# A gated cross-attention block with a mixture of experts: the first batch brought alone to its scores, the rest of its block behind it

## The chip, the cores and the metric

The kernel runs on one core of a Trainium2 chip. The core has five engines that work side by side and wait for each other through semaphores: TensorE (PE, matrix products, with PEld for its weight loads), VectorE (DVE), ScalarE (ACT), GpSimd (POOL) and SyncE (SP, which here only issues transfers). The metric is the device time of one execution in microseconds (us); a comparison takes the median of several runs. One execution is also recorded by the hardware profiler, and all rows quoted here are from such a record.

## The reference

Inputs are `x` of 16 batches x 128 rows x 128 features, a context of 16 x 77 x 96, and the weights, all in 32-bit floats. Cut to what matters:

```python
# 1. gated cross-attention, 16 heads of 8 features
h  = layernorm(x)
q  = h @ Wq.T + bq                       # [16, 128, 16 heads, 8]
kv = ctx_768 @ Wkv.T + bkv               # per head 8 key and 8 value features
k, v = kv[..., :8], kv[..., 8:]
att = softmax(q k^T / sqrt(8), over the 77 context rows)
x  = x + tanh(g_xattn) * ((att @ v) @ Wo.T + bo)
# 2. gated mixture of experts, 4 rounds, 4 experts, the best 2 of each row
cur = layernorm(x)
for r in range(4):
    w   = softmax of the two largest of (cur @ Wg[r] + bg[r]), zero elsewhere
    cur = cur + sum_e w[e] * (gelu(cur @ W1[e] + b1[e]) @ W2[e] + b2[e])
out = x + tanh(g_ffn) * cur
```

## The kernel before, in words

The 16 batches are tiles of 128 rows. They are prepared in four blocks of four (`BB = 4`, `NB = 4`): normalization, turning (transposing) `x` and the context, keys, queries and values are done for a block at a time. The order of the instructions on PE, DVE and ACT is the order of the program text (a manual schedule); POOL's is kept in program order too, by the wrapper `gp`. An engine takes its instructions strictly one after the other, so an instruction that waits holds up all behind it on that engine.

**The head, up to line 876.** Loads are issued from three queues: SP brings `x` and the context block by block, ACT the projection weights, and POOL the two bias rows of `wkT` and `wvT`. DVE clears both `vm` buffers (the values, spread out with zeros, one for even and one for odd blocks) and makes `hmask`, which picks a head's rows. `warm(n)` puts n products of a zero matrix on PE. Then, for the first block: `Wkv` and `Wq` are turned, and the first four contexts (`turn_ctx(0)`); `keys(0)` makes `kT`; `cols` is made by turning `cols_n`, the expert biases `b1` with the query bias `bq` as a last row; `stats_x` and `Norm.scale` find mean and 1/deviation for four tiles (the power -1/2 is taken on POOL); `norm_x(0)` applies them on DVE; `turn_x(0)` and `queries(0)` make `qT`. `spread_keys(b)` multiplies `kT` with `hmask` (`km`, on POOL), so that `scores(b)` can compute four heads by one product. `weights` is the softmax without its division: largest value (`mx`) and difference (`ex`) on DVE, exponential on ACT, in two halves. `values(0)` makes `vm[0]`. In the same stretch the second block's statistics and norm, its contexts and its keys are placed.

`spread_rows` (line 878) spreads small rows over all partitions: gate weights' biases, the two gates (`tg`), the attention's output bias (`bo_b`), and turns `Wo` and `Wg`. All its results lie in one PSUM bank.

**The attention loop, line 1039.** One turn for each batch b. A turn makes `km` of batch b+2, turns the weights of batch b (`turn_weights`, PE into `ps_tr`, copied by ACT to `exT`), makes the scores of b+1 between the two halves of that, starts the softmax of b+1, and multiplies the weights of b with ones and values (`attend`, `ps_av`); `over_sums` divides (`rs`, `oT`), and `put_out` of the next turn adds the result to `x`. Work of the later blocks and of the routing is hung into the turns by hand, through lists of functions at four places of a turn:

```python
    early[1] += [lambda: turn_x(1)]
    extra[2] += [lambda: queries(1)]
    extra[3] += [lambda: values(1)]
    for b in (0, 1, 2, 5, 6):
        behind[b] += [lambda: advance(constants, 1)]
```

`early` comes after the first half of the turned weights, `extra` after the second half, `amid` after `attend`, and `behind` at the end of the turn. `constants` are tables for the routing, made on POOL in five steps.

**PSUM.** The pool `p_m` (`bank`) has two banks, used in turn by nearly all products; `p_tr` (`bank_tr`) has two for `ps_tr`; `p_sc` (`banks2`) has two pairs for scores, which `warm` uses too. A bank is given to the next user when its last reader is done.

**The experts, from line 1082.** Eight phases (two halves of the rows, four rounds) go over pieces of 128 rows sorted by expert: two layers on PE (`ps_h`, `ps_y`), the gelu on ACT.

Of the kernel before, what the change touches and what calls it, by code (L numbers as in the profile page):

```python
# [31 lines left out]
P = 128  # L32
# [14 lines left out]
def gated_xattn_moe(  # L47
# [66 lines left out]
    def bank(name):  # L114
        return p_m.tile([P, 512], F32, tag="m", name=name)
# [3 lines left out]
    ctx_sb = keep.tile([M, B, C], F32, name="ctx_sb")  # L119
    wkv_n = const.tile([P, 2, C], F32, name="wkv_n")  # L120
    wq_n = const.tile([D, D], F32, name="wq_n")
    NCOL = E * NF + 1
    cols_n = const.tile([NCOL, P], F32, name="cols_n")

    wkT = const.tile([C + 1, D], F32, name="wkT")
    wvT = const.tile([C + 1, D], F32, name="wvT")

    nc.scalar.dma_start(wkv_n, Wkv.rearrange("(t p) c -> p t c", p=P))
    nc.scalar.dma_start(wq_n, Wq)
    wg_sb = const.tile([D, R, E], F32, name="wg_sb")  # L130
    nc.scalar.dma_start(wg_sb, Wg.rearrange("r d e -> d r e"))
    nc.scalar.dma_start(cols_n[E * NF : NCOL, :], bq.rearrange("(o d) -> o d", o=1))
    nc.scalar.dma_start(cols_n[0 : E * NF, :], b1.rearrange("e (c p) -> (e c) p", p=P))
    bkv_v = bkv.rearrange("(o h t d) -> o t h d", o=1, t=2, d=DH)
    ident = const.tile([P, P], F32, name="ident")
    make_identity(nc, ident)
    for t, w in ((0, wkT), (1, wvT)):
        gp.dma_start(
            w[C : C + 1, :].rearrange("o (h d) -> o h d", d=DH), bkv_v[:, t]
        )  # L140
    for i in range(NB):
        nc.sync.dma_start(
            x_sb[:, ts(i, BB), :], x[ts(i, BB)].rearrange("b l d -> l b d")
        )
        nc.sync.dma_start(
            ctx_sb[:, ts(i, BB), :], ctx_768[ts(i, BB)].rearrange("b m c -> m b c")
        )
# [51 lines left out]
    nc.vector.tensor_reduce(
        hmask,  # L200
        ident.rearrange("p (g k d) -> p k g d", k=HG, d=DH),
        AX.XY,
        ALU.add,
    )
# [475 lines left out]
    warm(9)  # L680
    ps = bank("ps_wkv")
    for t in range(2):
        tp(ps[:C, ts(t, P)], wkv_n[:, t, :], ident)
    tp(ps[:, 2 * P : 3 * P], wq_n, ident)
    for t, w in ((0, wkT), (1, wvT)):
        nc.vector.tensor_copy(
            w[0:C, :].rearrange("c (h d) -> c h d", d=DH),
            ps[:C, : 2 * D].rearrange("c (h t d) -> c t h d", t=2, d=DH)[:, t],
        )
    wqT = const.tile([D, D], F32, name="wqT")  # L690
    nc.scalar.copy(wqT, ps[:, 2 * P : 3 * P])
# [33 lines left out]

    xnTs = {}

    def turn_x(i):
        ps = bank("ps_xt")
        for j in range(BB):  # L730
            tp(ps[:, ts(j, P)], row(i * BB + j, 0, D), ident)
        xnTs[i] = awork.tile([P, TB], F32, tag="xnT", name="xnT")
        nc.scalar.copy(xnTs[i], ps)

    def queries(i):
        ps = bank("ps_q")
        mm(ps, wqT, xnTs.pop(i), start=True, stop=True)
        nc.scalar.activation(qT[i], ps, AF.Identity, bias=bqc)

    def values(i):  # L740
        ps = bank("ps_v")
# [94 lines left out]
    def put_out(b, oT, bank):  # L836
# [30 lines left out]
    warm(10)
    turn_x(0)
    warm(3)
    queries(0)  # L870
    warm(4)
    scs = scores(0, kms.pop(0))
    values(0)
    turn_ctx(1)
    ex = {0: weights(scs)}
    keys(1)

    def spread_rows():
# [7 lines left out]
        nc.scalar.activation(tg, rows_b[:, R * E : NROW], AF.Tanh)
        nc.vector.tensor_scalar(bo_b, ps[:, ts(1, D)], tg[:, 0:1], None, ALU.mult)
        nc.scalar.copy(woT, ps[:, ts(2, D)])
        wgT = const.tile([R * E, D], F32, name="wgT")
# [147 lines left out]
    extra[B - 1] += [begin]  # L1037
    o = {}
    for b in range(B):
        if b + 2 < B:  # L1040
            kms[b + 2] = spread_keys(b + 2)
        exT = awork.tile([M, NH, L], F32, tag="exT", name="exT")
        turn_weights(ex[b], exT, (0, 1))
        for f in early[b]:
            f()
        if b + 1 < B:
            scs = scores(b + 1, kms.pop(b + 1))
        turn_weights(ex.pop(b), exT, (2, 3))
# [29 lines left out]
        if b == 14:  # L1078
            load(0, stores)
# [280 lines left out]
```

## Time and profile before

| what | value |
|---|---|
| three runs | 449.91, 449.91 and 450.17 us; median 449.91 |
| the profiled execution | 448.24 us, of it 446.4 from the first to the last instruction (the span) |
| busy over the span | PE 430.0, DVE 346.5, ACT 274.8, POOL 214.4 us |
| mean granted clock of TensorE | 0.994 |
| head: up to the first turn's first `ps_tr` | 19.4 us |
| attention loop | 19.4 to about 114 us |
| experts | from about 114 us on |

In the rows below a number in front is the start in microseconds from the span's start, then the duration, the engine, the line, the instruction, what it writes and reads, and how often; in brackets the idle time before it and what ended it. A matrix product of 32-bit floats appears as two instructions (passes). PE's weight loads have rows of their own (PEld). Rows of the same group that follow each other are merged into one.

### The profile page before, as it was taken

How to read it: one execution, taken by the hardware profiler on the slowest of the kernel's cores; microseconds unless marked ns; L12 is line 12 of the kernel's file. 1: busy time of each engine (PE TensorE's matmuls, PEld its weight loads, DVE VectorE, ACT ScalarE, POOL GpSimd, SP SyncE). 2: the span in 40 equal slices, each digit the busy share in tenths (PEclk: the TensorE clock that was granted, in tenths of full speed). 3: DMA queues.
4: the chain of work that ended last, by engine and by line, in shares of the span. 5: the costliest groups of instructions: out<-in, count | busy, mean ns of one | idle time of the engine just before them, and what ended most of it. 6: DMA issues, size and time to landing. Idle time of an engine off the chain costs nothing.

```text
span 446.4 us, 12234 instructions
## 1 busy us (share of the span) xinstructions
PE 430.0 (96%) x4506; PEld 405.3 (91%) x4506; DVE 346.5 (78%) x918; ACT 274.8 (62%) x853; POOL 214.4 (48%) x249
## 2 busy tenths in 40 slices
PE   6899999998999999999999999999999999999991
PEld 6677888877899999999999999999999999999991
DVE  8489998998866996897698689858867986774561
ACT  2567766766655666566666656666665666666661
POOL 5561926157005934752592377158426814650061
PEclk9999999999999999999999999999999999999997
DMA  7520000012202301300130122014002201410000
GB/s 166 184 96 4 1 3 1 1 40 76 84 3 74 121 2 51 122 28 3 72 123 1 38 73 88 1 63 135 2 26 73 98 3 63 134 42 8 1 35 14
DMA packets 19553, 24.08 MB, mean 54 GB/s; under 512 B 3940, under 2 KB 16550, under 8 KB 19366
## 3 DMA queue, kind: packets, MB, share of 16 engines
q1 hardware_dynamic: 14868, 13.41, 9.6%
q0 software_dynamic: 3648, 9.71, 6.0%
q8 instruction: 36, 0.59, 0.5%
q10 hardware_dynamic: 978, 0.18, 0.2%
q14 instruction: 23, 0.19, 0.1%
HBM read 13.58 MB, written 9.71 MB: 52 GB/s over the span
## 4 chain that ended last, share of the span: by engine, by line
PE 71%; issue 9%; DVE 8%; POOL 6%; DMA 4%; ACT 1%; POOLq 0%; ACTq 0%; DVEq 0%
PE ps_y L262 28%; PE ps_h L262 28%; POOL out_dram L1124 4%; PE ps_av L262 4%; PE ps_tr L265 4%; DVE mx L791 2%; DMA wall<-in_L_ffn_W_dram 2%; DVE ex L795 2%; PE ps_c L265 2%; DVE rs L831 1%; PE sc L262 1%; DMA ctx_sb<-in_ctx_dram 1%; PE ps_bh L262 1%; DMA wq_n<-in_L_xattn_Wq_dram 1%; ACT exT L809 1%
## 5 line engine op out<-in xcount | busy, mean ns | idle before, releaser
L1096 ACT ACTIVATE hT<-ps_h,wb 128x128 f32<-128x128 f32 x512 | 145.9, 368 | 81.6 <-ACT hT L1096 56.7
L262 PE MATMUL ps_h<-curT,wb 128*128 128x128 f32 x1024 | 135.4, 275 | 0.7 <-ACT curT L379 0.7
L262 PE MATMUL ps_y<-wb,hT 128*128 128x128 f32 x1024 | 135.7, 276 | 0.0
L262 PEld LDWEIGHTS ps_h<-curT,wb 128*128 128x128 f32 x1024 | 124.6, 192 | 0.9 <-ACT curT L379 0.9
L262 PEld LDWEIGHTS ps_y<-wb,hT 128*128 128x128 f32 x1024 | 124.5, 192 | 0.0
L522 POOL DMA_INDIRECT sorted<-rows,pos_i x64 | 69.9, 1092 | 112.2 <-DVE start L515 49.3
L1015 DVE COPY wb<-wall 128x1028 f32 x128 | 105.4, 826 | 12.7 <-issue 6.5
L93 POOL TENSOR_TENSOR lp<-rows,wg_rows 128x512 f32<-128x512 f32 x48 | 75.3, 1593 | 29.7 <-DVE rows L1110 27.5
L1110 DVE SCALAR_TENSOR_TENSOR rows<-ps_y,pws,rows 128x128 f32<-128x128 f32 x126 | 43.6, 346 | 33.9 <-PE ps_y L262 33.9
L1096 ACT ACTIVATE hT<-ps_h,wall 128x128 f32<-128x128 f32 x160 | 45.7, 368 | 32.6 <-PE ps_h L262 32.6
L262 PE MATMUL ps_y<-wall,hT 128*128 128x128 f32 x320 | 43.1, 278 | 0.0
L262 PE MATMUL ps_h<-cx,wall 128*128 128x128 f32 x320 | 42.3, 275 | 0.0
L809 ACT COPY exT<-ps_tr 77x512 f32<-77x512 f32 x64 | 34.0, 581 | 13.4 <-PE ps_tr L265 13.1
L262 PEld LDWEIGHTS ps_y<-wall,hT 128*128 128x128 f32 x320 | 38.9, 192 | 2.7 <-ACT hT L1096 2.7
L262 PEld LDWEIGHTS ps_h<-cx,wall 128*128 128x128 f32 x320 | 38.9, 192 | 0.0
L265 PEld LDWEIGHTS ps_tr<-ident,ex 128*77 128x77 f32 x256 | 27.9, 147 | 10.1 <-ACT exT L809 7.8
L265 PE MATMUL ps_tr<-ident,ex 128*77 128x128 f32 x256 | 35.1, 280 | 1.1 <-ACT exT L809 1.1
L1124 POOL DMA_INDIRECT out_dram<-res,id_i x16 | 18.5, 1158 | 35.8 <-DVE res L1115 31.8
L419 DVE TENSOR_REDUCE lg<-lp 128x4 f32<-128x512 f32 x48 | 32.3, 674 | 3.4 <-POOL lp L93 3.4
L801 ACT ACTIVATE ex<-ex 128x616 f32<-128x616 f32 x32 | 23.0, 719 | 13.7 <-DVE ex L795 13.4
L791 DVE TENSOR_REDUCE mx<-sc 128x8 f32<-128x616 f32 x32 | 25.3, 790 | 5.8 <-PE sc L262 5.7
L795 DVE TENSOR_TENSOR ex<-sc,mx 128x616 f32<-128x616 f32 x32 | 25.4, 794 | 1.5
(170 smaller groups left out, 450.9 us busy)
## 6 DMA issues: line engine op xcount, KB each, us to landing
rows<-sorted SPq DMA_DIRECT2D x16, 528.0 KB
x_sb<-in_x_dram SPq DMA_DIRECT2D x4, 256.0 KB
wall<-in_L_ffn_W_dram SPq DMA_DIRECT2D x1, 1024.0 KB
wall<-in_L_ffn_W_dram SPq DMA_DIRECT2D x4, 256.0 KB
wg_rows<-wg_turned SPq DMA_DIRECT2D x1, 1024.0 KB
sorted<-rows,pos_i POOLq DMA_INDIRECT x64, 2.6
ctx_sb<-in_ctx_dram SPq DMA_DIRECT2D x4, 115.5 KB
out_dram<-res,id_i POOLq DMA_INDIRECT x16, 2.3
```

The costliest lines, as they stand in the source:

```text
L93: return lambda *a, **kw: tc.keep_in_program_order(f(*a, **kw))
L262: nc.tensor.matmul(*args, **kw)
L265: nc.tensor.transpose(*args)
L419: nc.vector.tensor_reduce(lgs[h][:, t, :], prods.pop((h, t)), AX.X, ALU.add)
L522: ins = nc.gpsimd.indirect_dma_start(out=sorted_rows[h], out_offset=bass.IndirectOffsetOnAxis(ap=pos_i[:, t : t + 1], axis=0), in_=rows[h] ...
L791: beats.append(nc.vector.tensor_reduce(mx, sv, AX.X, ALU.max))
L795: nc.vector.tensor_tensor(eu.rearrange("l (g h) m -> l g h m", h=HG), sv, mx.unsqueeze(3).to_broadcast([P, 2, HG, M]), ALU.subtract,)
L809: nc.scalar.copy(exT[:, ts(g, HG), :].rearrange("m h l -> m (h l)"), ps[:M, :])
L1015: nc.vector.tensor_copy(wb, wall[:, ds(e, 1), :].rearrange("p o n -> p (o n)"))
L1096: nc.scalar.activation(hT[:, fc, :], ps[:, ts(fc, P)], AF.Gelu_apprx_tanh, bias=wb[:, W_B + fc : W_B + fc + 1],)
L1110: return nc.vector.scalar_tensor_tensor(at, y, w, at, ALU.mult, ALU.add)
L1124: ins = nc.gpsimd.indirect_dma_start(out=out_rows, out_offset=bass.IndirectOffsetOnAxis(ap=id_i[:, t : t + 1], axis=0), in_=res, in_offset ...
```

## The change: what it does

It rearranges the head and the first turns of the loop.

- Loads. SP brings `x` of batch 0 alone first, then the first block's contexts, the other three tiles of `x`, then `wg_sb` and `b1` (both from ACT's queue before), then the later blocks. ACT's queue brings `Wkv`, the two bias rows (from POOL's queue before), `Wq`, and `bq` as a column by itself.
- A copy of one element (`junk`) is put ahead of ACT's other work.
- The norm of the first block is split: tile 0, tile 1, tiles 2 and 3, each with its own scale. Tiles 0 and 1 are applied on DVE, 2 and 3 on POOL. `turn_x` and `queries` take a range of tiles: tile 0, then tile 1, and in turn 0 of the loop tiles 2 and 3.
- `km` of batch 0 is made on DVE. Keys and queries of tile 0 come before `scores(0)`; queries of tile 1 stand in front of `values(0)`, and the copies of the values behind the softmax of batch 0.
- `warm(9)`, `warm(2)`, `warm(10)`, `warm(3)`, `warm(4)` become `warm(6)` and groups of 1 to 4 zero products (`warm_tr`, in `p_tr`'s banks) between the steps: 19 in place of 28.
- Into the loop move: `turn_ctx(1)` (turn 0), `keys(1)` (turn 1), `spread_rows`, `residual(0)`, and statistics and norm of block 1 (end of turn 0), the clearing of `vm[1]`, now on POOL (end of turn 0). `turn_x(1)` goes from turn 1 to turn 2, the routing constants' first three steps go one turn later, and two statistics of block 2 from turn 0 to turn 1. `km` of batch 3 is made at the end of turn 0. `blk` is cleared on POOL later, just ahead of the expert loads.
- `b1` is turned within `spread_rows`, in its bank, and copied from there to `wall`.

```diff
-    NCOL = E * NF + 1
-    cols_n = const.tile([NCOL, P], F32, name="cols_n")
+    cols_n = const.tile([E * NF, P], F32, name="cols_n")
+    bqc = const.tile([P, 1], F32, name="bqc")
...
     nc.scalar.dma_start(wkv_n, Wkv.rearrange("(t p) c -> p t c", p=P))
+    for t, w in ((0, wkT), (1, wvT)):
+        nc.scalar.dma_start(w[C : C + 1, :].rearrange("o (h d) -> o h d", d=DH), bkv_v[:, t])
     nc.scalar.dma_start(wq_n, Wq)
-    nc.scalar.dma_start(wg_sb, Wg.rearrange("r d e -> d r e"))
-    nc.scalar.dma_start(cols_n[E * NF : NCOL, :], bq.rearrange("(o d) -> o d", o=1))
-    nc.scalar.dma_start(cols_n[0 : E * NF, :], b1.rearrange("e (c p) -> (e c) p", p=P))
+    nc.scalar.dma_start(bqc, bq.rearrange("(d o) -> d o", o=1))
-    for t, w in ((0, wkT), (1, wvT)):
-        gp.dma_start(
-            w[C : C + 1, :].rearrange("o (h d) -> o h d", d=DH), bkv_v[:, t]
-        )
-    for i in range(NB):
+    nc.sync.dma_start(x_sb[:, 0, :], x[0])
+    nc.sync.dma_start(ctx_sb[:, 0:BB, :], ctx_768[0:BB].rearrange("b m c -> m b c"))
+    nc.sync.dma_start(x_sb[:, 1:BB, :], x[1:BB].rearrange("b l d -> l b d"))
+    nc.sync.dma_start(wg_sb, Wg.rearrange("r d e -> d r e"))
+    nc.sync.dma_start(cols_n, b1.rearrange("e (c p) -> (e c) p", p=P))
+    for i in range(1, NB):
...
-    for i in range(2):
-        nc.vector.memset(vm[i], 0.0)
+    nc.vector.memset(vm[0], 0.0)
...
-    gp.memset(blk, 0.0)
...
+    junk = const.tile([1, 1], F32, name="junk")
+    nc.scalar.copy(junk, zero[0:1, 0:1])
+    def warm_tr(n):
+        ps = bank_tr("ps_warm")
+        for _ in range(n):
+            mm(ps[:, :P], zero, zero, start=True, stop=True)
...
+    def turn_wq():
+        ps = bank_tr("ps_wq")
+        tp(ps[:, :P], wq_n, ident)
+        nc.scalar.copy(wqT, ps[:, :P])
...
-    turn_ctx(0)
-    warm(2)
-    keys(0)
-    ps = bank("ps_cols")
-    tp(ps[:, :NCOL], cols_n, ident[:NCOL, :NCOL])
-    nc.scalar.copy(cols, ps[:, :NCOL])
-    nc.scalar.copy(
-        wall[:, :, W_B:WW], cols[:, 0 : E * NF].rearrange("p (e c) -> p e c", c=NF)
-    )
-    for j in range(BB):
-        stats_x(0, j)
-    norms[0].scale()
-    kms = {0: spread_keys(0), 1: spread_keys(1)}
-    stats_x(1, 0)
-    stats_x(1, 1)
-    norm_x(0, nc.vector)
-    stats_x(1, 2)
-    stats_x(1, 3)
-    norms[1].scale()
-    norm_x(1, gp)
-    load_experts()
-    warm(10)
-    turn_x(0)
-    warm(3)
-    queries(0)
-    warm(4)
-    scs = scores(0, kms.pop(0))
-    values(0)
-    turn_ctx(1)
-    ex = {0: weights(scs)}
-    keys(1)
+    norms0 = Norm(1, "b"), Norm(1, "c"), Norm(BB - 2, "d")
+    norms0[0].stats(0, x_sb[:, 0, :])
+    norms0[0].scale()
+    nc.vector.tensor_reduce(
+        hmask, ident.rearrange("p (g k d) -> p k g d", k=HG, d=DH), AX.XY, ALU.add
+    )
+    warm(6)
+    norms0[0].apply(0, row(0, 0, D), x_sb[:, 0, :], nc.vector)
+    turn_wkv()
+    turn_ctx(0)
+    warm_tr(1)
+    turn_wq()
+    turn_x(0, 0, 1)
+    warm_tr(2)
+    norms0[1].stats(0, x_sb[:, 1, :])
+    norms0[1].scale()
+    keys(0)
+    warm_tr(1)
+    queries(0, 0, 1)
+    warm_tr(3)
+    for j in range(2, BB):
+        norms0[2].stats(j - 2, x_sb[:, j, :])
+    norms0[2].scale()
+    kms = {0: spread_keys(0, nc.vector), 1: spread_keys(1)}
+    norms0[1].apply(0, row(1, 0, D), x_sb[:, 1, :], nc.vector)
+    scs = scores(0, kms.pop(0))
+    turn_x(0, 1, 2)
+    warm_tr(2)
+    queries(0, 1, 2)
+    values(0, False)
+    warm_tr(4)
+    ex = {0: weights(scs)}
+    values_done(0)
+    for j in range(2, BB):
+        norms0[2].apply(j - 2, row(j, 0, D), x_sb[:, j, :], gp)
+    gp.memset(blk, 0.0)
+    load_experts()
...
-    spread_rows()
-    residual(0)
-    early[1] += [lambda: turn_x(1)]
+    def spread_more():
+        kms[3] = spread_keys(3)
+    extra[0] += [lambda: turn_x(0, 2, BB), lambda: queries(0, 2, BB), lambda: turn_ctx(1)]
+    extra[1] += [lambda: keys(1)]
+    behind[0] += [spread_rows, spread_more, lambda: residual(0)]
+    for j in range(BB):
+        behind[0] += [lambda j=j: stats_x(1, j)]
+    behind[0] += [lambda: norms[1].scale(), lambda: norm_x(1, gp), lambda: gp.memset(vm[1], 0.0)]
+    early[2] += [lambda: turn_x(1)]
     extra[2] += [lambda: queries(1)]
     extra[3] += [lambda: values(1)]
-    for b in (0, 1, 2, 5, 6):
+    for b in (1, 2, 3, 5, 6):
         behind[b] += [lambda: advance(constants, 1)]
...
-            behind[b - 4 + j] += [lambda i=i, j=j: stats_x(i, j)]
+            behind[max(b - 4 + j, 1)] += [lambda i=i, j=j: stats_x(i, j)]
```

More of the change, by code (lines that the diff above doesn't have):

```diff
@@ L128, in gated_xattn_moe @@
     nc.scalar.dma_start(wkv_n, Wkv.rearrange("(t p) c -> p t c", p=P))
+    wg_sb = const.tile([D, R, E], F32, name="wg_sb")
+    bkv_v = bkv.rearrange("(o h t d) -> o t h d", o=1, t=2, d=DH)
+    for t, w in ((0, wkT), (1, wvT)):
+        nc.scalar.dma_start(w[C : C + 1, :].rearrange("o (h d) -> o h d", d=DH), bkv_v[:, t])
     nc.scalar.dma_start(wq_n, Wq)
-    wg_sb = const.tile([D, R, E], F32, name="wg_sb")
-    nc.scalar.dma_start(wg_sb, Wg.rearrange("r d e -> d r e"))
-    nc.scalar.dma_start(cols_n[E * NF : NCOL, :], bq.rearrange("(o d) -> o d", o=1))
-    nc.scalar.dma_start(cols_n[0 : E * NF, :], b1.rearrange("e (c p) -> (e c) p", p=P))
-    bkv_v = bkv.rearrange("(o h t d) -> o t h d", o=1, t=2, d=DH)
+    nc.scalar.dma_start(bqc, bq.rearrange("(d o) -> d o", o=1))
     ident = const.tile([P, P], F32, name="ident")
     make_identity(nc, ident)
-    for t, w in ((0, wkT), (1, wvT)):
-        gp.dma_start(
-            w[C : C + 1, :].rearrange("o (h d) -> o h d", d=DH), bkv_v[:, t]
-        )
-    for i in range(NB):
+    nc.sync.dma_start(x_sb[:, 0, :], x[0])
[4 more added lines that the diff above has]
+    for i in range(1, NB):
         nc.sync.dma_start(
@@ L195, in gated_xattn_moe @@
     vm = [akeep.tile([M, BB, HG * (D + DH)], F32, name=f"vm{i}") for i in range(2)]
-    for i in range(2):
-        nc.vector.memset(vm[i], 0.0)
[L199 to L203, printed above, removed]
-    )
+    nc.vector.memset(vm[0], 0.0)
     ctxT = akeep.tile([C + 1, B, M], F32, name="ctxT")
@@ L677, in warm, with turn_wkv @@
             mm(ps[:, 0, :P], zero, zero, start=True, stop=True)
[L680 to L689, printed above, removed]
-    wqT = const.tile([D, D], F32, name="wqT")
-    nc.scalar.copy(wqT, ps[:, 2 * P : 3 * P])
+    junk = const.tile([1, 1], F32, name="junk")
+    nc.scalar.copy(junk, zero[0:1, 0:1])
+    wqT = const.tile([D, D], F32, name="wqT")
+    def warm_tr(n):
+        ps = bank_tr("ps_warm")
+        for _ in range(n):
+            mm(ps[:, :P], zero, zero, start=True, stop=True)
+    def turn_wkv():
+        ps = bank("ps_wkv")
+        for t in range(2):
+            tp(ps[:C, ts(t, P)], wkv_n[:, t, :], ident)
+        for t, w in ((0, wkT), (1, wvT)):
+            nc.vector.tensor_copy(
+                w[0:C, :].rearrange("c (h d) -> c h d", d=DH),
+                ps[:C, : 2 * D].rearrange("c (h t d) -> c t h d", t=2, d=DH)[:, t],
+            )
[3 more added lines that the diff above has]
+        nc.scalar.copy(wqT, ps[:, :P])
     kT = akeep.tile([D, B, M], F32, name="kT")
     qT = [akeep.tile([D, TB], F32, name=f"qT{i}") for i in range(NB)]
-    cols = const.tile([P, NCOL], F32, name="cols")
-    bqc = cols[:, E * NF : NCOL]
     norms = {}
@@ L726, in gated_xattn_moe, with turn_x, queries, values @@
     xnTs = {}
-    def turn_x(i):
+    def turn_x(i, lo=0, hi=BB):
         ps = bank("ps_xt")
-        for j in range(BB):
+        for j in range(lo, hi):
             tp(ps[:, ts(j, P)], row(i * BB + j, 0, D), ident)
+        at = slice(lo * P, hi * P)
         xnTs[i] = awork.tile([P, TB], F32, tag="xnT", name="xnT")
-        nc.scalar.copy(xnTs[i], ps)
-    def queries(i):
+        nc.scalar.copy(xnTs[i][:, at], ps[:, at])
+    def queries(i, lo=0, hi=BB):
         ps = bank("ps_q")
[L737 to L741, printed above, removed]
+        at = slice(lo * P, hi * P)
+        mm(ps[:, at], wqT, xnTs.pop(i)[:, at], start=True, stop=True)
+        nc.scalar.activation(qT[i][:, at], ps[:, at], AF.Identity, bias=bqc)
+    pss_v = {}
+    def values(i, done=True):
+        ps = pss_v[i] = bank("ps_v")
         for j in range(BB):
             mm(ps[:M, ts(j, D)], ctxT[:, i * BB + j, :], wvT, start=True, stop=True)
+        if done:
+            values_done(i)
+    def values_done(i):
+        ps = pss_v.pop(i)
         for j in range(BB):
@@ L751, in values, with spread_keys @@
             )
-    def spread_keys(b):
+    def spread_keys(b, eng=gp):
         km = awork.tile([D, HG, M], F32, tag="km", name="km")
-        gp.tensor_tensor(
+        eng.tensor_tensor(
             km,
@@ L843, in put_out @@
         )
-    turn_ctx(0)
-    warm(2)
-    keys(0)
-    ps = bank("ps_cols")
-    tp(ps[:, :NCOL], cols_n, ident[:NCOL, :NCOL])
-    nc.scalar.copy(cols, ps[:, :NCOL])
-    nc.scalar.copy(
-        wall[:, :, W_B:WW], cols[:, 0 : E * NF].rearrange("p (e c) -> p e c", c=NF)
-    )
-    for j in range(BB):
-        stats_x(0, j)
-    norms[0].scale()
-    kms = {0: spread_keys(0), 1: spread_keys(1)}
-    stats_x(1, 0)
-    stats_x(1, 1)
-    norm_x(0, nc.vector)
-    stats_x(1, 2)
-    stats_x(1, 3)
-    norms[1].scale()
-    norm_x(1, gp)
-    load_experts()
-    warm(10)
-    turn_x(0)
-    warm(3)
-    queries(0)
-    warm(4)
-    scs = scores(0, kms.pop(0))
-    values(0)
-    turn_ctx(1)
-    ex = {0: weights(scs)}
-    keys(1)
+    norms0 = Norm(1, "b"), Norm(1, "c"), Norm(BB - 2, "d")
[3 more added lines that the diff above has]
+        hmask, ident.rearrange("p (g k d) -> p k g d", k=HG, d=DH), AX.XY, ALU.add
+    )
+    warm(6)
+    norms0[0].apply(0, row(0, 0, D), x_sb[:, 0, :], nc.vector)
+    turn_wkv()
+    turn_ctx(0)
+    warm_tr(1)
[4 more added lines that the diff above has]
+    norms0[1].scale()
+    keys(0)
+    warm_tr(1)
[17 more added lines that the diff above has]
+    gp.memset(blk, 0.0)
+    load_experts()
     def spread_rows():
@@ L882, in spread_rows @@
         mm(ps[:, ts(1, D)], ones, bo_row, start=True, stop=True)
+        tp(ps[:, 32 : 32 + E * NF], cols_n, ident[: E * NF, : E * NF])
         tp(ps[:, ts(2, D)], wo_n, ident)
@@ L888, in spread_rows @@
         nc.scalar.copy(woT, ps[:, ts(2, D)])
+        nc.scalar.copy(
+            wall[:, :, W_B:WW],
+            ps[:, 32 : 32 + E * NF].rearrange("p (e c) -> p e c", c=NF),
+        )
         wgT = const.tile([R * E, D], F32, name="wgT")
@@ L1039, in gated_xattn_moe @@
     for b in range(B):
-        if b + 2 < B:
+        if b + 2 < B and b + 2 not in kms:
             kms[b + 2] = spread_keys(b + 2)
@@ L1063, in gated_xattn_moe @@
         if b == B - 1:
-            junk = const.tile([1, 1], F32, name="junk")
             nc.scalar.activation(junk, zero[0:1, 0:1], AF.Gelu_apprx_tanh)
```

## The prediction

> **What bounds the kernel now.** The page first: busy time of each engine.
>
> ```profile
> PE 430.0 (96%) x4506; PEld 405.3 (91%) x4506; DVE 346.5 (78%) x918; ACT 274.8 (62%) x853; POOL 214.4 (48%) x249
> ```
>
> TensorE (PE) is the long engine, but where it idles or only multiplies zeros decides here. So next the busy time by stretch (columns: stretch, its length, then PE, PEld, DVE, ACT, POOL).
>
> ```profile
> 0.00:20.00 20.00, 15.75 (x106) 13.13 (x107) 13.05 (x35) 6.72 (x17) 10.34 (x23) 1.00 0.71 195
> 20.00:66.00 46.00, 45.42 (x754) 36.15 (x753) 40.82 (x87) 33.04 (x66) 24.38 (x79) 1.00 0.07 25
> 112.00:440.00 328.00, 324.50 (x2952) 320.23 (x2941) 249.99 (x693) 204.78 (x714) 156.68 (x121) 1.00 0.16 53
> ```
>
> From 20 us on PE is full (45.42 of 46, 324.5 of 328), so microseconds won before it shift everything behind. Between 66 and 112 the chain of waits runs through VectorE (DVE), but it starts at the row `rs` at 65.92, which waits for PE: that stretch shifts too. What counts is when the first batches get through, so the timeline of the head (start, duration, engine, line, operation):
>
> ```profile
> 6.29 1.28 ACT L691 ACT_TABLE_LOAD   x1 [6.29 <-DVE wvT L686]
> 8.10 1.04 POOL L93 TENSOR_TENSOR rstda<-rstda,half 128x4 f32<-128x4 f32 x1 [3.44 <-DVE rstda L251]
> 9.18 1.91 DVE L255 TENSOR_SCALAR rows<-x_sb,mva,rstda 128x128 f32<-128x128 f32 x4 [0.35 <-POOL rstda L93]
> 11.45 0.60 PE L265 MATMUL ps_xt<-ident,rows 128*128 128x128 f32 x4
> 12.72 1.12 PE L262 MATMUL ps_q<-xnT,wqT 128*128 128x512 f32 x2
> 14.72 0.87 PE L262 MATMUL sc<-km,qT 32*128 32x308 f32 x8
> 15.54 0.80 DVE L791 TENSOR_REDUCE mx<-sc 128x8 f32<-128x616 f32 x1 [3.44 <-PE sc L262]
> 19.40 1.04 PE L265 MATMUL ps_tr<-ident,ex 128*77 128x128 f32 x8
> 20.05 0.35 DVE L887 TENSOR_SCALAR bo_b<-ps_rows,tg 128x128 f32<-128x128 f32 x1 [0.27 <-ACT tg L886]
> 20.49 0.27 ACT L888 COPY woT<-ps_rows 128x128 f32<-128x128 f32 x1 [0.47 <-PE ps_tr L265]
> 25.11 1.10 PE L265 MATMUL ps_tr<-ident,ex 128*77 128x128 f32 x8
> 30.98 1.10 PE L265 MATMUL ps_tr<-ident,ex 128*77 128x128 f32 x8
> 36.74 1.10 PE L265 MATMUL ps_tr<-ident,ex 128*77 128x128 f32 x8
> ```
>
> The first softmax (`mx`) starts at 15.54, after four tiles were normed, turned and multiplied. Turn 0 of the attention loop begins with its first `ps_tr` at 19.40, turns 1, 2, 3 at 25.11, 30.98, 36.74. Rows L691 and L888 show a habit of this kernel: ScalarE (ACT) starts reading a PSUM bank only when DVE, ahead of it in the program, has finished with that bank. Last the waits; SyncE's tell when loads landed:
>
> ```profile
> SPq L145 <- DMA wkv_n<-in_L_xattn_Wkv_dram: 1.7, 1, 1.7
> SPq L145 <- DMA wq_n<-in_L_xattn_Wq_dram: 0.2, 1, 0.2
> ```
>
> The issues behind these waits ran at 3.85 and 4.84, so `wkv_n` (96 KB, issued 0.72) landed at 3.8 and `wq_n` (64 KB, issued 1.25) at 4.8.
>
> **The change, step by step.** I walk the new order with durations of this profile.
>
> *Norm of tile 0.* `x[0]` (64 KB, first on SP, issued near 0.73) lands between 3.0 (by the stretches of 1 us, the first 250 KB of all loads had moved by then) and 3.85, the time of the larger `wkv_n`; I take 3.4, and DVE's first `vm` fill ends at 3.4 anyway. Statistics 0.45 and scale 0.17 (rows at 6.14 and 7.84), power 1.04 on GpSimd (POOL, free by 2.9 since the two bias loads left it), one apply 0.34: 5.5. The `wkT` and `wvT` copies follow (0.46): 6.0. They hold the PSUM bank that `turn_x` needs, so PE turns x at 6.1. `turn_wq` lies ahead: `wq_n` is now ACT's fourth load, issued near 2.3 instead of 1.25; 3.6 us later is 5.9, just hidden. If it takes 1 us longer, that is 1 us lost. The table load (1.28) moves to about 3.2 on an idle ACT: hidden.
>
> *PE to the scores.* Turn 0.27, two zero products 0.50 (a product is two passes of 0.125: 20 passes in 2.50 at 9.11), keys 0.76, one more 0.25, queries of one tile 0.40 (a 128x128 product pair takes 0.38 to 0.49), three more 0.75: 9.0. Beside it `kT` is copied by 8.1 and `qT` by 8.7. The new `spread_keys(0)` on DVE costs 0.40, half of `ex` (616 elements, 0.80). Its bound is the neighbour: in the row at 9.18 two of the four applies took 0.64 and 0.74 instead of 0.34, ending with POOL's two `km` products beside them. The third power (1.04) then runs from 7.8 to 8.85, so `km` ends between 8.5 (no contention) and 10.0 (DVE waits for the power and for POOL's `km` of batch 1); I take 9.6, nearer to the contended rows. Scores 0.85: **`mx` at 10.45, 5.1 us earlier.**
>
> The Trainium skill, SBUF — State Buffer, section "SBUF: two separate sides", calls the pair that DVE and GpSimd share an exclusive lock held for a whole instruction. The stretched applies agree; by it alone `km` ends at 9.3 or 10.0.
>
> *Turn 0.* From `mx` to the second exponential's end took 3.93 (15.54 to 19.47): 14.4. The four `vm` copies (0.75) now stand between it and ACT's `exT` copies: 15.15. PE, done with four zero products at 13.8, has turned groups 0 and 1; groups 2 and 3 wait for banks that `exT` frees. The four copies, 0.55 each with one wait of 0.1: 17.4. New in this turn, in series between PE and ACT: `xnT` of two tiles 0.38, `queries` 0.55, `qT` 0.45: 18.9; `turn_ctx(1)` beside it. `attend` 1.93: 20.85. Moved behind it, `spread_rows` (18.48 to 19.4 before): 0.9. Turn 1 starts at 21.75 against 25.11: **3.35 ahead.** The turn takes 1.75 us more after `mx` than before.
>
> *Turn 1.* ACT's `tg` waits for `rows_b`, behind `rs` and `oT` (0.96 and 0.29) on DVE: 22.65. `bo_b` ends at 23.05, then by the bank habit `woT`, the moved `wall` biases and `wgT` (0.27, 0.20, 0.25): 23.8. Queued behind them is `exT`, ready at 22.45; PE's groups 2 and 3 wait for it until 24.4 and end at 25.5. Keys (new here, 0.52), `ps_o` 0.46, `attend` 1.93: turn 2 at 28.4 against 30.98: **2.55 ahead.**
>
> *Turn 2* takes over `turn_x(1)`, 0.44 of PE, from turn 1: **2.1 ahead at turn 3.** Its input is late: statistics of batch 1 now run on DVE behind `bo_b` (four by 0.43: 24.75), scale, power (1.04: 26.0), four applies on POOL (3.13: 29.15). PE asks at 28.4 + 1.04 = 29.45. Slack 0.3.
>
> *Covered.* The second `vm` fill leaves DVE (1.87) for POOL, about 2.0 by the 1232-element fill (1.12); it stands before `km` of batch 4, done near 32.6, wanted near 35: slack 2.4. If that cover goes, it costs its excess. The `blk` fill (0.31) is off any path; the expert loads are wanted at 109. The routing constants go one turn later; the long step (4.9) then ends near 41.5, when the power of batch 2 is due: `km` of batch 6 keeps about 0.4 of the 0.95 it has now. SP's queue carries `wg_sb` and `cols_n` ahead of `x` of batch 1, wanted at 23. The `bq` column by DMA replaces a transpose and copy; it has until 8.2. Fewer zero products: 28 become 19.
>
> **Rivals.**
>
> *TensorE stays slow (slower).* The first zero products are slow: 18 passes take 3.79 us from 1.05 (0.21 each), 20 take 2.50 from 9.11 (0.125 each), while the granted clock reads 1.00 throughout; the last three of the first group, from 4.34, are already quick. Before, nine products run unbroken to 4.84; now six end at 3.6, and then come transposes, one product, and waits of up to 0.7. If a pass stays at 0.21, PE work of about 3 us from 6.1 to the scores and 3 us behind them until turn 0 costs 70% more: 4.2 us, so 447.8 + 4.2 = 452.0. It decides against the change once more than 2.1 us of that is lost, that is if the slow state lasts beyond the scores. One late window (to about 7.8) costs 1.0. Against: after an idle 2.3 us (5.95 to 8.26) the products at 9.11 were fast, and the longest gap now is shorter. Chance 0.09.
>
> The Trainium skill, TensorE: Matmul & The Clock Gate, Part 1, has the clock doubling after about 3.4 us of sustained work and dropping after as much idleness; Part 4 says transposes do not count as work. The trace's switch near 4.3, 3.2 us after the first product, agrees with the first; no run here shows the second yet.
>
> *POOL takes it back (no change).* With 0.3 us of slack at `turn_x(1)`, each microsecond by which POOL's batch-1 norm is later is lost. Contention of the kind at 9.18 (0.3 to 0.4 on an instruction) on six POOL instructions would cost 1.8 - 0.3 = 1.5: 449.3. For: POOL was idle 4.0 us before `bo_b`, now it has a queue. Against: most of DVE's work there reads PSUM. Chance 0.13.
>
> *The gain is kept (faster still).* If `km` is not contended (0.4 to 0.6 back) and ACT's late copies in turn 1 are hidden (1.35 back), 4.0 remain: 445.9. Chance 0.13.
>
> *The loads do not come first.* If `x[0]` or `wq_n` lands 1 us late, 448.8; inside the forecast's spread. Chance of the forecast with it 0.65.
>
> **The numbers.** The profiled execution took 448.24 us (span 446.4 and 1.8 around it); the median of the three runs, 449.91, is 1.67 above it, and I carry the difference unchanged. 448.24 - 2.1 = 446.1, so **447.8** as a median. The forecast's own spread is 446.6 to 449.2 (`km` 1.1 early or 0.4 late, loads 1.0 late). For 8 in 10 I reach down to 445.7 (gain kept) and up to 450.2, which takes in POOL and one late clock window but not the fully slow TensorE. About 0.2% (0.9 us) is what a measurement of this kernel can tell from no change. Faster by more: 0.60 of the forecast's 0.65, 0.13, and 0.05 of POOL's: 0.78. Within: 0.05, 0.06 of POOL's and 0.01 of the clock's: 0.12. Slower: the rest of the clock's and POOL's: 0.10.
>
> **What would show it.** Right: `mx` first near 10.5, `ps_tr` of turns 1, 2 and 3 near 21.8, 28.4 and 34.6, busy time from 112 on unchanged, span near 444.3. ACT's `exT` of turn 1 should wait behind `wgT`. Wrong: zero passes still 0.2 apart after 7 us (clock); PE waiting for POOL `rows` at `ps_xt` in turn 2, or for `km` in turns 3 to 5 (POOL); `sc` waiting for `km` beyond 10 (contention); turn 3 at the old 36.7 (nothing kept).

## The result, and the profile after

| | before | after |
|---|---|---|
| median of 6 runs each, side by side | 449.86 us (448.20 to 450.17) | 444.11 us (443.72 to 446.01) |
| profiled execution, of it the span | 448.24, 446.4 us | 444.04, 442.3 us |
| mean granted clock of the profiled execution | 0.994 | 0.993 |

The ratio is 0.9883, interval 0.9861 to 0.9905: 5.75 us faster, where 2.1 were forecast (447.8, range 445.7 to 450.2). The direction was right; the size was wrong, and the time fell below the range.

The busy times of the page hardly differ from before, and a stretch of 328 us that begins near the experts in both has nearly the same PE busy time (324.25 now, 324.50 then). First the line of the page, then that of the windows (columns: stretch, length, PE, PEld, DVE, ACT, POOL, granted clock, DMA share, GB/s):

```profile
PE 427.3 (97%) x4492; PEld 403.8 (91%) x4492; DVE 343.7 (78%) x918; ACT 275.7 (62%) x857; POOL 216.7 (49%) x251
```

```profile
108.00:436.00 328.00, 324.25 (x2944) 319.93 (x2933) 249.09 (x693) 204.97 (x714) 156.63 (x121) 1.00 0.16 54
```

So the gain was made ahead of that, in the head and the first turns. The timeline of after, up to the first largest value:

```profile
4.04 0.58 POOL L93 TENSOR_TENSOR rstdb<-rstdb,half 128x1 f32<-128x1 f32 x1 [1.04 <-DVE rstdb L244]
4.66 0.34 DVE L248 TENSOR_SCALAR rows<-x_sb,mvb,rstdb 128x128 f32<-128x128 f32 x1 [0.51 <-POOL rstdb L93]
4.98 0.40 ACT L716 COPY ctxT<-ps_ct 96x308 f32<-96x308 f32 x1
5.12 0.28 DVE L687 COPY wvT<-ps_wkv 96x128 f32<-96x128 f32 x1
5.22 0.42 PE L258 MATMUL ps_wq<-ident,wq_n 128*128 128x128 f32 x1
5.43 0.18 PEld L258 LDWEIGHTS ps_xt<-ident,rows 128*128 128x128 f32 x1 [0.19 <-ACT ctxT L716]
5.43 0.42 PE L258 MATMUL ps_xt<-ident,rows 128*128 128x128 f32 x1
5.69 0.61 PE L255 MATMUL ps_warm<-zero 128*128 128x128 f32 x4
6.13 0.69 PE L255 MATMUL ps_k<-ctxT,wkT 97*128 97x308 f32 x2
6.66 0.38 PE L255 MATMUL ps_warm<-zero 128*128 128x128 f32 x2
6.88 0.39 PE L255 MATMUL ps_q<-xnT,wqT 128*128 128x128 f32 x2
7.09 0.70 POOL L93 TENSOR_TENSOR rstdd<-rstdd,half 128x2 f32<-128x2 f32 x1 [0.45 <-DVE rstdd L244]
...
7.30 0.48 DVE L768 TENSOR_TENSOR km<-kT,hmask 128x308 f32<-128x308 f32 x1 [0.29 <-ACT kT L726]
7.93 0.80 PE L255 MATMUL sc<-km,qT 32*128 32x308 f32 x8
8.76 0.80 DVE L803 TENSOR_REDUCE mx<-sc 128x8 f32<-128x616 f32 x1 [0.21 <-PE sc L255]
```

`mx` starts at 8.76, where before it was 15.54 and the forecast 10.45. Three things can be read here. Each PE row's duration reaches into the next row: the keys last 0.69, but the next products start 0.53 after them (6.66 - 6.13). `km` on DVE takes 0.48 although POOL's power ran beside it. And what ended the wait of `ps_xt` at 5.43 is ACT's copy of the contexts (`ctxT`, 4.98 to 5.38). Next the loop's turns, by their first `ps_tr`, and what ACT does at the start of turn 1:

```profile
20.02 1.04 PE L258 MATMUL ps_tr<-ident,ex 128*77 128x128 f32 x8
21.31 0.27 ACT L909 COPY woT<-ps_rows 128x128 f32<-128x128 f32 x1 [0.47 <-DVE bo_b L908]
...
21.53 0.25 ACT L915 COPY wgT<-ps_rows 16x128 f32<-16x128 f32 x1
21.69 1.05 ACT L821 COPY exT<-ps_tr 77x512 f32<-77x512 f32 x2
22.31 1.14 PE L258 MATMUL ps_tr<-ident,ex 128*77 128x128 f32 x8 [0.53 <-ACT exT L821]
26.01 1.10 PE L258 MATMUL ps_tr<-ident,ex 128*77 128x128 f32 x8
27.44 0.14 PEld L258 LDWEIGHTS ps_xt<-ident,rows 128*128 128x128 f32 x1 [0.24 <-POOL rows L93]
32.43 1.10 PE L258 MATMUL ps_tr<-ident,ex 128*77 128x128 f32 x8
```

Turns 1, 2 and 3 stand 5.1, 5.0 and 4.3 ahead of before (25.11, 30.98, 36.74). Both places that the prediction worked out for a loss are there: `exT` queues behind `woT`, `wall` and `wgT`, and at 27.44 PE has waited 0.24 for POOL's `rows`. The first cost some tenths less than forecast, the second some tenths more. The 4.3 at turn 3 is the 4.2 between the profiled executions (448.24 - 444.04). The other 1.6 of the 5.75 is not in these two profiles at all, since the profiled execution of before was 1.6 below its median, that of after 0.1.

### The profile page after: what moved, and what is told of

Read it like the earlier page. It is cut to its first block, busy times and chain, and to the rows that moved or that the text cites. A ratio compares the mean times of both kernels' runs of the same rounds, so it can differ in the third digit from the quotient of the medians.

```text
span 442.3 us, 12215 instructions
## 1 busy us (share of the span) xinstructions
PE 427.3 (97%) x4492; PEld 403.8 (91%) x4492; DVE 343.7 (78%) x918; ACT 275.7 (62%) x857; POOL 216.7 (49%) x251
## 4 chain that ended last, share of the span: by engine, by line
PE 72%; issue 9%; DVE 9%; POOL 6%; DMA 2%; ACT 1%; POOLq 0%; DVEq 0%; SPq 0%; ACTq 0%
PE ps_y L255 28%; PE ps_h L255 28%; POOL out_dram L1156 4%; PE ps_av L255 3%; PE ps_tr L258 3%; DVE mx L803 2%; DVE ex L807 2%; PE ps_c L258 2%; DVE rs L843 1%; PE sc L255 1%; PE ps_warm L255 1%; PE ps_bh L255 1%; DMA rows<-sorted 1%; DMA sorted<-rows,pos_i 1%; POOL rows L93 1%
## 5 line engine op out<-in xcount | busy, mean ns | idle before, releaser
L821 ACT COPY exT<-ps_tr 77x512 f32<-77x512 f32 x64 | 34.0, 582 | 12.2 <-PE ps_tr L258 11.9
```

The lines of the kernel that those rows point to most:

```text
L821: nc.scalar.copy(exT[:, ts(g, HG), :].rearrange("m h l -> m (h l)"), ps[:M, :])
```

## The experiments

Two questions were open: where the missing 1.6 of the medians lies, and which terms of the head were mis-sized. The theory for the first was the clock of TensorE, slow in most executions of before and not in the profiled one; the rival, that profile and median differ by something constant.

### Before again, unchanged

Edit: none.

> The kernel before, unchanged, against itself. Its runs lie on two levels, 448.2 and 449.8. Theory of the clock: TensorE's slow state at the start lasts one period longer in most executions, because TensorE idles from 5.95 to 8.26 us. Then most runs are near 449.8, and in a profile of one of those the zero passes that start near 9 us take 0.2 us each and the scores come 1 to 2 us later than 14.72. Rival, something elsewhere (a transfer, the end): the head of such a profile is like the one already seen (passes of 0.125 from 9.11, scores at 14.72), and the 1.7 us lie in another stretch.

Measured: 450.16 (448.25 to 451.81, 12 runs), ratio 1.001 (0.9991 to 1.003). Together with 30 further executions of before that were taken beside them, these are 42. They lie on three levels, and the mean granted clock goes with them: 11 at 448.2 to 448.8 (clock 0.993 or 0.994), 23 at 449.8 to 450.4 (0.989 to 0.991), 8 at 451.3 to 451.8 (0.987). The first profile of before is of the first level, this one (449.83) of the second. Its windows of 1 us:

```profile
7.00:8.00 1.00, 0.00 (x0) 0.00 (x0) 0.90 (x7) 0.99 (x3) 0.00 (x0) 1.00 0.94 254
8.00:9.00 1.00, 0.74 (x2) 0.30 (x2) 0.76 (x5) 0.16 (x1) 0.90 (x1) 0.74 0.84 236
9.00:10.00 1.00, 1.00 (x4) 0.61 (x4) 0.82 (x4) 0.51 (x3) 0.19 (x2) 0.50 0.41 91
10.00:11.00 1.00, 1.00 (x6) 1.00 (x6) 0.97 (x4) 0.19 (x1) 1.00 (x2) 0.50 0.80 199
11.00:12.00 1.00, 1.00 (x8) 1.00 (x7) 0.69 (x4) 0.00 (x0) 0.48 (x2) 0.55 1.01 395
```

The third number from the right is the granted clock. PE idles from 6.3 to 8.26, and from about 8.5 to 11.9 the clock is half. The timeline of the same execution gives the price:

```profile
8.26 1.16 PE L262 MATMUL ps_k<-ctxT,wkT 97*128 97x308 f32 x2 [1.95 <-DVE st L247]
9.57 3.59 PE L262 MATMUL ps_warm<-zero 128*128 128x128 f32 x20
16.27 0.87 PE L262 MATMUL sc<-km,qT 32*128 32x308 f32 x8
```

The 20 zero passes took 2.50 in the first profile, the scores stood at 14.72: they come 1.55 later, and so do turns 1 to 3 (26.66, 32.53, 38.29). That is the step between the levels. The rival of a constant difference falls: the difference belongs to executions, not to profiles.

### Before with one idle stretch filled

```diff
     turn_ctx(0)
-    warm(2)
+    warm(9)
     keys(0)
```

> The kernel before with nine zero products in place of two behind the first context turns, so that TensorE multiplies in its idle 5.95 to 8.26 us. Theory of the clock: the slow state ends early in most executions, the median goes to 448.2 (ratio 0.996). Rival, the level has another cause: median 449.8 as before, or up to 0.6 later if the seven products run slowly (0.42 each) and hold the keys up.

Measured: 449.11 (448.24 to 449.74, 12 runs), ratio 0.9981 (0.9963 to 0.9999). No execution is left at 451.3 to 451.8; half are at 448.2 to 448.7, half at 449.6 to 449.7, the profiled one (449.56) among these. So part of the cause was met, and the windows show where the rest is:

```profile
17.00:18.00 1.00, 0.17 (x1) 0.17 (x2) 0.97 (x3) 1.00 (x5) 0.00 (x0) 1.00 0.69 200
19.00:20.00 1.00, 1.00 (x6) 0.80 (x6) 0.09 (x1) 0.83 (x2) 0.00 (x0) 0.56 0.02 5
20.00:21.00 1.00, 1.00 (x7) 1.00 (x6) 0.44 (x2) 0.41 (x3) 0.21 (x1) 0.50 0.00 0
```

PE's second idle stretch (0.17 busy between 17 and 18) is followed by a half clock, from about 19.1 to 22.5.

### Before with both idle stretches filled

```diff
-    warm(2)
+    warm(9)
...
     turn_ctx(1)
+    ps = bank_tr("ps_warm")
+    for _ in range(4):
+        mm(ps[:, :P], zero, zero, start=True, stop=True)
     ex = {0: weights(scs)}
```

> The kernel before with both of TensorE's early idle stretches filled: seven products more before the keys, four behind the second block's contexts (idle from 16.9 to 17.8). With the first alone half of the runs lay at 448.3 to 448.7 and half at 449.6 to 449.7, and in a profile of the latter the passes from 19.2 to 22.7 were slow. Theory of the clock: now nearly all runs lie at 448.2 to 448.9, median 448.4, ratio 0.9965. Rival, other causes: the mixture stays, median 449.1.

Measured: 448.23, ratio 0.9959 (0.9943 to 0.9974), and all six runs lie between 448.21 and 448.40 at a clock of 0.993 to 0.995: one level. Two lines of its timeline:

```profile
14.72 0.87 PE L262 MATMUL sc<-km,qT 32*128 32x308 f32 x8
16.72 1.10 PE L262 MATMUL ps_warm<-zero 128*128 128x128 f32 x8
```

The scores stand at 14.72 as in the first profile of before; nothing of the order was improved. Eleven zero products take off 1.88 (before ran at 450.11 beside it) by keeping the clock up. From 448.23 to after's 444.11 are 4.12, close to the 4.20 by which the two profiles differ. This settles the first question.

### After without the zero products in the gaps

Left out: the six calls of `warm_tr` (13 products; `warm(6)` stays).

> The changed kernel without its 13 zero products in the gaps; only the first six stay. Theory of the clock: TensorE's gaps become idle, the slow state lasts past the scores in most executions, and the products and turns of the head cost 70% more: 445.8 to 446.5 (1.7 to 2.4 more than 444.1). Rival, the zero products only stand in front of real ones: TensorE reaches the scores up to 0.5 us earlier and the first turned weights up to 0.5 earlier: 443.3 to 444.1.

Measured: 446.14 (444.75 to 447.61, 7 runs), ratio 0.9926 (0.9897 to 0.9956), 2.0 slower than after. The profiled execution (445.35, clock 0.986), timeline and one window:

```profile
7.54 1.34 PE L255 MATMUL sc<-km,qT 32*128 32x308 f32 x8 [0.94 <-DVE km L768]
11.94 1.91 PE L258 MATMUL ps_tr<-ident,ex 128*77 128x128 f32 x8
```

```profile
8.00:9.00 1.00, 1.00 (x9) 0.18 (x1) 0.10 (x1) 0.00 (x0) 1.00 (x2) 0.50 0.99 228
```

The scores start 0.39 earlier than in after, with less queued ahead of them, and then the clock is half from about 7.7 to 14.5: they take 1.34 instead of 0.80, turn 1 begins at 21.00 instead of 20.02, and the time is 1.3 above that of after's profile (445.35 for 444.04). The order alone brings the median under before (446.14 for 450.06); the zero products are worth another 2.0. Only this one execution shows the half clock. The other six, at 444.75 to 447.61, have mean clocks of 0.990 to 0.995 that do not follow their times (447.61 at 0.993, 446.14 at 0.995), so what holds the slowest of them up is not shown.

### After with one norm for the four tiles

```diff
-    norms0 = Norm(1, "b"), Norm(1, "c"), Norm(BB - 2, "d")
-    norms0[0].stats(0, x_sb[:, 0, :])
-    norms0[0].scale()
+    norm0 = Norm(BB, "b")
+    for j in range(BB):
+        norm0.stats(j, x_sb[:, j, :])
+    norm0.scale()
...
```

The other statistics, scales and applies of the first block go over to this one norm.

> The changed kernel with one norm for the first block's four tiles (four statistics, one power of 128x4) ahead of the first apply, in place of three norms. Theory, the split of the norm carries the early scores: three more statistics (0.42 each) and a power of 1.04 in place of 0.58 stand before tile 0, 1.7 us in all, of which 0.2 to 0.5 come back behind it: 445.3 to 445.8. Rival, the loads (Wq, the other three tiles) and the keys set the pace anyway: 444.1 to 444.5.

Measured: 448.19 (447.24 to 448.89, 12 runs), ratio 0.9958 (0.994 to 0.9976), 4.1 slower than after and 2.4 beyond what was expected at most. Its timeline:

```profile
4.68 0.29 DVE L240 BATCH_NORM_STATS2 st<-x_sb 128x6 f32<-128x128 f32 x1 [0.92 <-DMA x_sb<-in_x_dram]
6.27 1.04 POOL L93 TENSOR_TENSOR rstdb<-rstdb,half 128x4 f32<-128x4 f32 x1 [3.28 <-DVE rstdb L244]
7.84 0.45 PE L258 MATMUL ps_xt<-ident,rows 128*128 128x128 f32 x1 [2.21 <-DVE rows L248]
12.23 1.41 PE L255 MATMUL sc<-km,qT 32*128 32x308 f32 x8
```

The wait for three more tiles, their statistics and the larger power put `turn_x` 2.4 later (7.84 for 5.43). Then PE, idle for 2.2, is slow: from the turn to the scores 4.4 instead of 2.5. So the delay in front was larger than expected, and the 1.9 behind it, PE at its slow rate, had not been expected at all. Turn 3 is at 37.33, later than before's 36.74: in this profile the whole gain of the order is gone. Of the 4.3 by which the scores are late, 2.4 come from the later tile 0 and 1.9 from the slow PE.

### After with the first block's `x` in one load

```diff
-    nc.sync.dma_start(x_sb[:, 0, :], x[0])
+    nc.sync.dma_start(x_sb[:, 0:BB, :], x[0:BB].rearrange("b l d -> l b d"))
     nc.sync.dma_start(ctx_sb[:, 0:BB, :], ctx_768[0:BB].rearrange("b m c -> m b c"))
-    nc.sync.dma_start(x_sb[:, 1:BB, :], x[1:BB].rearrange("b l d -> l b d"))
```

> The changed kernel with x of batches 0 to 3 as one load of 256 KB, as before, in place of tile 0 alone first. Theory, the small first load carries part of the gain: the statistics of tile 0 start near 4.6 (when the three other tiles landed in the kernel with one norm) instead of 3.33, 1.3 us later, and all up to the scores with them: 445.4, up to 446.5 if TensorE's wait for tile 0 then brings the slow state. Rival, DVE's fill of vm (to 3.4) and the weights hide it: 444.1 to 444.5.

Measured: 445.80 (444.39 to 446.51, 6 runs), ratio 0.9893 (0.9867 to 0.9919). The profiled execution took 445.21:

```profile
4.80 0.29 DVE L239 BATCH_NORM_STATS2 st<-x_sb 128x6 f32<-128x128 f32 x1 [1.40 <-DMA x_sb<-in_x_dram]
6.65 0.28 DVE L686 COPY wvT<-ps_wkv 96x128 f32<-96x128 f32 x1
6.69 0.30 PE L257 MATMUL ps_xt<-ident,rows 128*128 128x128 f32 x1 [0.48 <-DVE rows L247]
8.63 0.86 POOL L93 TENSOR_TENSOR rstdd<-rstdd,half 128x2 f32<-128x2 f32 x1 [0.45 <-DVE rstdd L243]
```

The statistics start 1.47 later (4.80 for 3.33), `turn_x` 1.26, turn 3 (33.55) 1.12: against the first runs of after the load of 64 KB alone first is worth 1.1 to 1.7, against after again (below: 444.53, turn 3 at 32.80), which ran beside this one, 0.8 to 1.3. Two more things are to be seen. PE turns `x` while the copy of `wvT` runs: the copies do not hold it, though the prediction had assumed that they do. And the power beside DVE's `km` took 0.86 instead of 0.70.

### After with the second block's work back in front

Contexts, keys, `spread_rows`, residual, statistics and norm of block 1 and the clearing of `vm[1]` stand ahead of turn 0 again; queries of tiles 2 and 3 stay in turn 0. `turn_x(1)`, the first three steps of the routing constants and `km` of batch 3 go back to their old turns.

> The changed kernel with the second block's contexts and keys, the spread rows, the residual and the second block's norm in front of turn 0 again; the early scores of batch 0 stay. Theory, moving them behind is a part of the gain: contexts, keys and spread rows (0.3 + 0.5 + 0.9 of TensorE, with ScalarE's copies between) delay turn 0 by 2.5 to 3.4 and give 1.7 to 2.2 back in turns 0 to 2: 445.0 to 446.0. Rival, the early scores are all of it and the moved work costs the same in either place: 443.9 to 444.4.

Measured: 445.97 (445.64 to 446.41, 5 runs), ratio 0.9904 (0.9881 to 0.9927). The size is as expected, the place is partly another. The scores are at 8.02 and turn 1 at 21.08, 1.1 later than in after; turn 2 is 2.5 later (28.52), by a wait in turn 1 (PE, then POOL):

```profile
24.11 0.80 PE L255 MATMUL sc<-km,qT 32*128 32x308 f32 x8 [1.50 <-POOL km L93]
```

```profile
18.42 3.12 POOL L93 TENSOR_SCALAR rows<-x_sb,mva,rstda 128x128 f32<-128x128 f32 x4
21.48 1.91 POOL L93 MEMSET vm<- 77x2176 f32 x1
```

`km` of batch 2 stood behind the norm of block 1 and the clearing of `vm[1]` on POOL's queue and ran at 23.35. So putting the rest of the block behind is worth 1.9 against the first runs of after, and 1.4 against after again (444.53), which ran beside it. In the profiles 1.1 is lost before turn 1 by the work itself, and 0.8 more stands at turn 3 (34.27 for 32.43), the net of POOL's wait and of what changed turns.

### After again, and with the longer power

After unchanged, then with tile 0's power over four columns:

```diff
-    norms0 = Norm(1, "b"), Norm(1, "c"), Norm(BB - 2, "d")
+    norms0 = Norm(BB, "b"), Norm(1, "c"), Norm(BB - 2, "d")
+    gp.memset(norms0[0].mv, 1.0)
```

> The changed kernel, unchanged. Theory of the clock: with TensorE kept busy its slow state is over by the scores in most executions; the runs lie near 444.1 with a few at 446, the kernel before again on 448.3, 450.1 and 451.5. Rival: both kernels have the same mixture of levels, so that several runs of the changed one lie at 446 to 447.5 and the median difference is only the 4.1 of the two profiled executions.

> The changed kernel with tile 0's power -1/2 taken over four columns instead of one (three of them filled with ones, unused). It changes one price alone: 1.04 instead of 0.58. Theory, the power lies in the path to the scores, and that I priced it by the 128x4 row was an error of 0.46: all from tile 0's apply on 0.4 to 0.5 later, scores 0.4 to 0.5 later than 7.93 to 8.30, time 444.9 (0.4 more than 444.5). Rival, Wq's load and turn (done at 5.64) or the clock set the start of turn_x: 444.5.

Measured: the copy 444.53 (443.73 to 444.67, 4 runs), ratio 0.9863 (0.9835 to 0.989), with scores at 8.30 and turn 3 at 32.80 in its profile, where the four zero passes behind `turn_x` took 0.97 and not 0.61 as in the first; the longer power 443.97 (443.92 to 444.42, 5 runs), ratio 0.9866 (0.9848 to 0.9884). The timeline of the latter:

```profile
4.13 1.04 POOL L93 TENSOR_TENSOR rstdb<-rstdb,half 128x4 f32<-128x4 f32 x1 [1.10 <-DVE rstdb L244]
5.70 0.30 PE L258 MATMUL ps_xt<-ident,rows 128*128 128x128 f32 x1 [0.32 <-ACT wqT L695]
```

The power is 0.46 longer, `turn_x` starts 0.27 later, the scores stand at 8.09, between those of the two runs of after (7.93 and 8.30). The theory that the power's size explains 0.4 of the missed gain falls. The apply ends 0.55 later than in after (5.55 for 5.00), but in after PE takes `x` only at 5.43, when ACT's copy of the contexts is done, so about half of the delay is covered. After without the zero products has `turn_x` at 5.43 too, with PE idle for 0.25 before it: it was not PE's own queue that held `x`.

### Two steps further

First, `turn_ctx(1)` ahead of the queries in turn 0, and `spread_rows` split, so that its copies of `woT`, `wall` and `wgT` come behind `exT` of turn 1. Then also the values of the first block copied by DVE, so that ACT is free for `exT` of turn 0:

```diff
-    extra[0] += [lambda: turn_x(0, 2, BB), lambda: queries(0, 2, BB), lambda: turn_ctx(1)]
-    extra[1] += [lambda: keys(1)]
+    extra[0] += [lambda: turn_x(0, 2, BB), lambda: turn_ctx(1), lambda: queries(0, 2, BB)]
+    extra[1] += [spread_rest, lambda: keys(1)]
...
-    values_done(0)
+    values_done(0, nc.vector.tensor_copy)
```

> The changed kernel with two orders changed: in turn 0 the second block's contexts stand between turn_x and queries, where TensorE waits 0.7 us for ScalarE's xnT, and in turn 1 woT, wall's biases and wgT are copied behind the exT copies instead of ahead of them, where TensorE waits 0.5 to 1.0. Theory, these waits set the pace of turns 0 and 1: 0.5 and 0.5 to 0.8 less, 442.8 to 443.2. Rival, DVE (statistics of block 1, then the softmax of batch 2) sets the pace of turn 1 and only turn 0's part remains or less: 443.5 to 444.1.

> The version with two orders changed, and besides the copies of the first block's values on DVE, which waits 1.3 us for the scores of batch 1, instead of on ScalarE, where they stand 0.73 us in front of the exT copies that TensorE waits for. Theory, ScalarE sets the pace of turn 0: 0.5 to 0.7 less than 443.4, 442.7 to 442.9. Rival, DVE is then late with the softmax of batch 1, which is wanted at the start of turn 1: 443.4 or more.

Measured: the first 443.38 (443.15 to 443.96, 5 runs), ratio 0.9848 (0.9825 to 0.9871); both 442.51 (442.39 to 443.15, 5 runs), ratio 0.9835 (0.9817 to 0.9853), the lowest median here. The first lies between its theory and its rival, the second 0.2 below its theory. The timeline of both:

```profile
11.75 0.87 DVE L758 COPY vm<-ps_v 77x128 f32<-77x128 f32 x4
12.49 1.05 ACT L821 COPY exT<-ps_tr 77x512 f32<-77x512 f32 x2
18.64 1.04 PE L258 MATMUL ps_tr<-ident,ex 128*77 128x128 f32 x8
```

`exT` of turn 0 starts at 12.49 instead of 13.20 in after, turn 1 at 18.64 instead of 20.02, and turn 3 (31.02 for 32.43) keeps the 1.4. The medians of both and of after differ by 1.6; the intervals of the first step and of after overlap, so that step by itself is shown by its profile (turn 1 at 19.31, turn 3 at 31.70) more than by its times.

## Why the prediction was wrong in size

The forecast missed by 3.7 (447.8 - 444.1), in two steps of about equal weight.

**The level: 1.6.** "I carry the difference unchanged" was the step that failed. The 1.67 between profiled execution and median of before was not an offset of profiles but the slow clock behind PE's idle stretches, absent in the profiled execution (both fillings, 450.11 to 448.23). The change puts zero products into such gaps, and five of after's six runs lie within 0.4 of its profiled execution. *TensorE stays slow* was the right mechanism laid on the wrong kernel: it was a cost of before that went, not one of after that came. Its argument against ("after an idle 2.3 us (5.95 to 8.26) the products at 9.11 were fast") rested on one execution of the minority, 11 of 42. After without the gap products is 2.0 slower, and its profiled execution has the half clock.

The Trainium skill, TensorE: Matmul & The Clock Gate, Part 1, gives the clock a window of about 3.4 us; the half clock of 8.5 to 11.9 and of 19.1 to 22.5 in two executions agrees. The advice of the Trainium skill on the same page, section "Why this matters for your kernels", to keep idle gaps below some 3 us is not narrow enough by these runs, where gaps of 2.0 and 0.9 were followed by a half clock.

**The walk: 2.1.** Profiled execution against profiled execution, 446.1 was forecast and 444.04 came. By the prediction's own steps:

- *Norm of tile 0*: `turn_x` at 5.43, not 6.1 (0.67). The power on one column takes 0.58, not the 1.04 of the row for four; but the longer power moved `turn_x` by 0.27 only, and the time not measurably. The other 0.4 is the term of 0.46 for the copies of `wkT` and `wvT`, which had no ground: the run with `x` in one load turns `x` beside such a copy. The copy that `turn_x` did wait for is that of the contexts, to 5.38.
- *PE to the scores*: 7.93 - 5.43 = 2.50, where the sum had 2.9 for PE and 0.6 more for `km`. The 0.6 was the choice "nearer to the contended rows"; `km` took 0.48. It was POOL's power that was stretched in another run (0.86 for 0.70), and DVE's apply of tile 1 (0.84 for 0.34). The other 0.4 comes from summing durations: keys 0.76 and queries 0.40 were entered whole, and PE goes on after 0.53 and 0.22.
- *Turn 0* was right: from `mx` to turn 1 11.26 measured (20.02 - 8.76), 11.30 forecast.
- *Turn 1*: 5.99, not 6.65. `exT` did queue behind `woT`, `wall` and `wgT`, as forecast, but the first of those starts only 0.38 before `exT`, where their durations (0.72) had been summed. The rest again is PE's rows overlapping.
- *Turn 2*: 6.42, not 6.20. Where a slack of 0.3 was forecast at `turn_x(1)`, PE waited 0.24: POOL's rows came last. *POOL takes it back* named this place rightly, at a sixth of its price.

*The gain is kept* came nearest (445.9, on the old level 1.67: on the new one 444.3). Both its conditions held in the main: `km` not contended, half of ACT's copies hidden.

**Not settled.** One run of after took 446.01 at a clock of 0.990; by the levels above that fits the slow clock, but no trace of it was taken. Half the runs with `x` in one load were at 446.4 to 446.5 with a clock reading of 0.995, and one without the gap products was at 447.61 with 0.993; the recorded clock does not explain these. A slow start that lasts longer, as in the run with one norm, would fit, but was not shown for them. Why an idle of 2.0 is followed by the half clock in some executions and not in others was not tried. Nor were the early table load, `km` on DVE and the order of the later loads tried singly.

## What to carry to other kernels

Before a change is sized from one profile, see on which level of the runs that profile lies, by its time and mean clock, and name what the other level is made of: the change may remove it. Along a pipelined engine add start-to-start distances of rows, not durations. Where work is moved behind the first tile, fill TensorE's gaps until it runs without pause, and check what then stands on each queue ahead of the operands of the next product.

## What the runs showed of the hardware

- A half clock of about 3.4 us follows idle stretches of TensorE of 2.0 us, and even of 0.9 us (before with one stretch filled), in some executions only; one execution of after without gap products, idle for 0.94 before its scores, had twice that length (7.7 to 14.5). With zero products in both stretches of before, all six runs lay within 448.21 to 448.40, the level without it.
- A slow start is not recorded as such: in the run with one norm four passes of zeros take 1.06 and the scores 1.41, at a granted clock that reads 1.00. Durations of known passes tell more than that column.
- The power on GpSimd takes 0.58, 0.70 and 1.04 for one, two and four columns.
- The Trainium skill, SBUF — State Buffer, section "SBUF: two separate sides", lets the second of two instructions wait for the whole of the first, where a DVE instruction with two SBUF inputs meets a GpSimd instruction that reads SBUF. In after `km` (DVE, two SBUF tiles in) started 0.2 after a power on POOL, with 0.5 of that left, and took 0.48 in all, so it does not agree with a whole wait. DVE's apply of tile 1, one SBUF tile in, took 0.84 instead of 0.34 beside POOL's `km`. No run isolates either pair.
